# Where the group statistics and variances of the next image stand in the instruction order of an attention kernel

## The chip, the cores and the metric

The kernel runs on one core of one Trainium2 chip. The metric is the time of one execution in microseconds of the device. The time before is the median of four runs, 3243.06 us (3242.06 to 3248.0). The engines are called as in the profile: PE (matrix), PEld (its weight loads), DVE (vector), ACT (scalar), POOL (GpSimd), SP (the queue that issues most transfers).

## What is computed

Two layers of the same form over 4 images of 32 x 32 positions and 768 channels, all in float32:

```python
def _gn(v, G=32, eps=1e-5):
    g = v.reshape(B_, H_, W_, G, C_ // G)
    m = jnp.mean(g, axis=(1, 2, 4), keepdims=True)
    s = jnp.var(g, axis=(1, 2, 4), keepdims=True)
    return ((g - m) / jnp.sqrt(s + eps)).reshape(v.shape)

x = x + _L0_conv_ref(_gn(x), ...)
x = x + _L1_conv_ref(_gn(x), ...)
```

Each layer normalises 32 groups of 24 channels, makes q, k and v for 12 heads of 64, adds a bias of relative positions to the 1024 x 1024 scores of each head, takes a softmax, weighs v and projects the result, which is added to x. The second layer has biases on q, k and v and scales q once more.

## The kernel before

The four images of two layers make eight turns, called images 0 to 7 here; the result of one layer goes through DRAM (mid) and is the input of an image four turns later. An image has six pairs of heads (pair 0 to 5), and a pair has eight steps (n = 0 to 7), one for each block of 128 positions: 384 steps, all in one loop (L1005). The order is written out by hand: the order of the statements is the order of the instructions on each engine, and an engine runs its own in that order, waiting on semaphores for the others.

In a step, POOL makes the biases of the step two ahead (L536, tiles sc), PE the scores of the next step (L550), DVE adds the two and takes the row minimum (L562), ACT takes exponentials (L566) and, after a reciprocal on DVE (L573, in divide), scales the rows (L576). DVE transposes the scaled scores of the present step in blocks (L582, tile tb); SP sends them to DRAM (td<-tb, L584) and reads them back in another arrangement (pt<-td, L593) for PE to weigh v (L611), after which DVE evicts into attn (L620, L622).

Into these steps the loop lays the rest. Groups of matmuls (pj for q and k, pv for values, oa to od for the projection of the image before) follow the plans at L990 to L1001. Most groups are crossed: a first half of matmuls, then later a second half. To keep the second half from being moved up, DVE makes a tiny reduce of one column of the group's weights onto itself (between, L346: "wa<-wa", "wv<-wv" and so on): it waits for the first half, and the second half waits for it. These are the ordering instructions. The loop runs them for the groups in held at the start of the next step (L1048 to L1051), but not in steps 2 and 6. All groups take PSUM buffers of tag m, of which there are two; a group's buffer is free when DVE or ACT has evicted it (od: L736, then L733; oc: L733, then L736 twice, the last of which writes oy).

In step 7 the plan is the second half of an oc group or none, an od group, and the first half of the next q and k group (pj<-xn,wa). In step 0 it is the next od group, the second half of that pj group and a values group.

The norm of an image is made while the image before it runs. Its statistics (stats, L210 to L217: bn_stats of 512 columns each, then one bn_aggr) are put into at_stats for a step and run near the end of that step (L1116). At pair 3 the groups are summed on 32 x 32 blocks: group_means at the end of step 6 (L285, L286 and spread at L279, L280), squares on POOL (L290, L291), group_variances in step 7 (L279, L280, transposes L295 and L296, a sum L297, then the root on ACT, L298, which loads another table first), and inverses in step 0 of pair 4 (L301, L302). Group_variances and inverses stand behind the exponentials of their step and ahead of its matmul groups and transposes (L1070).

## Time and profile before

| What | Value |
|---|---|
| median of four runs | 3243.06 us |
| the profiled execution's own time | 3248.0 us |
| its span, first to last instruction | 3246.2 us |
| PE busy | 3218.7 us (99%) |
| DVE busy | 2578.9 us (79%) |
| ACT busy | 2093.4 us (64%) |
| POOL busy | 2572.1 us (79%) |
| DMA, mean rate | 317 GB/s |
| L298 table load, one | 1.283 us, 7 times |
| L214 bn_stats, one | 0.67 us (median), 96 times |

How to read it: busy times are sums of recorded instruction spans, and matmuls overlap in the record. A row of waits has the engine and line that waited, what ended the wait, the microseconds in total, the number of waits, and the longest. A row of the timeline has the start, the time taken, engine, line, operation, output and inputs, and in brackets the idle time of the engine before it and what ended it. L numbers are lines of the kernel.

### The profile page before, as it was taken

How to read it: one execution, taken by the hardware profiler on the slowest of the kernel's cores; microseconds unless marked ns; L12 is line 12 of the kernel's file. 1: busy time of each engine (PE TensorE's matmuls, PEld its weight loads, DVE VectorE, ACT ScalarE, POOL GpSimd, SP SyncE). 2: the span in 40 equal slices, each digit the busy share in tenths (PEclk: the TensorE clock that was granted, in tenths of full speed). 3: DMA queues.
4: the chain of work that ended last, by engine and by line, in shares of the span. 5: the costliest groups of instructions: out<-in, count | busy, mean ns of one | idle time of the engine just before them, and what ended most of it. 6: DMA issues, size and time to landing. Idle time of an engine off the chain costs nothing.

```text
span 3246.2 us, 63998 instructions
## 1 busy us (share of the span) xinstructions
PE 3218.7 (99%) x24800; PEld 1856.7 (57%) x24800; DVE 2578.9 (79%) x4085; ACT 2093.4 (64%) x3098; POOL 2572.1 (79%) x1364
## 2 busy tenths in 40 slices
PE   8999999999999999999999999999999999999999
PEld 5565556555555556555565555555565555555554
DVE  6888778887888877788777887778777788777785
ACT  4777766676566666667656676666766567665662
POOL 6888967789787797878978889777897778977762
PEclk9999999999999999999999999999999999999999
DMA  5998888999989998899988999789988899888996
GB/s 189 349 347 318 312 309 306 331 337 331 320 298 340 337 326 317 295 338 345 326 303 310 344 336 338 285 302 335 325 324 301 298 340 331 311 312 300 324 336 253
DMA packets 386847, 1028.84 MB, mean 317 GB/s; under 512 B 31344, under 2 KB 73200, under 8 KB 337392
## 3 DMA queue, kind: packets, MB, share of 16 engines
q1 hardware_dynamic: 370992, 997.33, 86.2%
q10 hardware_dynamic: 15552, 27.43, 2.3%
q8 instruction: 196, 3.21, 0.4%
q14 instruction: 107, 0.88, 0.1%
HBM read 566.93 MB, written 457.70 MB: 316 GB/s over the span
## 4 chain that ended last, share of the span: by engine, by line
PE 93%; DVE 3%; DMA 2%; issue 1%; ACT 0%; POOL 0%; SPq 0%; DVEq 0%; POOLq 0%
PE pj L357 22%; PE av L611 20%; PE s L550 20%; PE pv L357 11%; PE pj L385 4%; PE oa L357 3%; PE ob L357 3%; PE oc L357 3%; PE tp L488 2%; PE pv L441 2%; PE o L833 1%; PE od L719 1%; DVE tb L582 1%; DMA td<-tb 1%; DMA pt<-td 1%
## 5 line engine op out<-in xcount | busy, mean ns | idle before, releaser
L536 POOL TENSOR_TENSOR sc<-rel 128x1024 f32<-128x1024 f32 x768 | 1944.5, 2559 | 534.7 <-DVE tb L582 415.5
L576 ACT ACTIVATE sc<-sc,sm 128x1024 f32<-128x1024 f32 x768 | 841.0, 1143 | 592.6 <-DVE sm L573 478.5
L562 DVE CUSTOM_DVE_ANT_0 sc<-s,sc 128x1024 f32<-128x1024 f32 x768 | 910.7, 1225 | 338.2 <-PE s L550 325.0
L566 ACT ACTIVATE sc<-sc,sm 128x1024 f32<-128x1024 f32 x768 | 877.3, 1144 | 257.7 <-DVE sm L562 255.1
L582 DVE STREAM_TRANSPOSE tb<-sc 128x1024 f32<-128x1024 f32 x768 | 911.5, 1231 | 14.1 <-DMA td<-tb 14.1
L550 PE MATMUL s<-k,q 64*128 64x512 f32 x3072 | 736.4, 596 | 0.5 <-DVE k L401 0.5
L611 PE MATMUL av<-pt,v 128*64 128x256 f32 x6144 | 684.9, 381 | 1.2 <-DMA pt<-td 1.2
L611 PEld LDWEIGHTS av<-pt,v 128*64 128x64 f32 x6144 | 433.6, 137 | 281.7 <-issue 38.9
L550 PEld LDWEIGHTS s<-k,q 64*128 64x128 f32 x3072 | 285.0, 187 | 296.6 <-issue 263.5
L357 PEld LDWEIGHTS pv<-wv,xn 64*128 64x128 f32 x4608 | 271.3, 188 | 35.5 <-issue 29.4
L357 PE MATMUL pv<-wv,xn 64*128 64x128 f32 x4608 | 273.8, 272 | 0.5 <-DVE wv L346 0.5
L357 PE MATMUL pj<-xn,wa 64*128 64x512 f32 x1152 | 266.9, 595 | 4.7 <-DVE wa L346 2.6
L357 PE MATMUL pj<-s,wc 64*128 64x512 f32 x576 | 262.8, 589 | 0.6 <-DVE wc L346 0.6
L357 PE MATMUL pj<-s,w 64*128 64x512 f32 x576 | 262.8, 589 | 0.6 <-DVE v L459 0.6
L357 PE MATMUL pj<-xn,w 64*128 64x512 f32 x1152 | 263.2, 589 | 0.0
L357 PEld LDWEIGHTS pj<-xn,wa 64*128 64x128 f32 x1152 | 111.5, 188 | 142.0 <-issue 116.2
L357 PEld LDWEIGHTS pj<-xn,w 64*128 64x128 f32 x1152 | 112.0, 187 | 135.2 <-issue 133.1
L459 DVE TENSOR_TENSOR v<-pv,v 128x512 f32<-128x512 f32 x216 | 140.2, 686 | 59.4 <-ACT v L461 42.5
L493 ACT COPY t<-tp 128x512 f32<-128x512 f32 x96 | 56.2, 586 | 159.1 <-PE tp L488 159.0
L511 ACT COPY rel<-raw 32x256 f32<-32x256 f32 x384 | 154.7, 403 | 3.6
L357 PEld LDWEIGHTS pv<-wv,s 64*128 64x128 f32 x2304 | 137.0, 188 | 24.2 <-issue 16.9
L357 PEld LDWEIGHTS pj<-s,wc 64*128 64x128 f32 x576 | 105.8, 187 | 68.6 <-issue 64.6
(134 smaller groups left out, 3394.0 us busy)
## 6 DMA issues: line engine op xcount, KB each, us to landing
td<-tb SPq DMA_DIRECT2D x384, 1024.0 KB, 5.3
pt<-td SPq DMA_DIRECT2D x382, 1024.0 KB, 8.3
tdr<-t ACTq DMA_DIRECT2D x96, 256.0 KB, 5.4
wa<-in_wqk SPq DMA_DIRECT2D x48, 384.0 KB, 4.1
wc<-in_wqk SPq DMA_DIRECT2D x48, 384.0 KB, 5.7
wv<-in_wv SPq DMA_DIRECT2D x24, 768.0 KB, 12.0
xn<-in_x SPq DMA_DIRECT2D x48, 256.0 KB, 5.5
res<-in_x SPq DMA_DIRECT2D x48, 256.0 KB, 5.4
```

The source lines that it names most:

```text
L357: nc.tensor.matmul(to, lhsT=w, rhs=x, start=at == half == 0, stop=at == 0 and half == 1)
L385: nc.tensor.matmul(t[:, h, :], lhsT=w[rows, c, :], rhs=x[c][rows, :], start=(c == 0), stop=(c == NB - 1),)
L441: nc.tensor.matmul(t[:, h, b, :], lhsT=s4[c][rows, b * P : (b + 1) * P], rhs=w22[rows, c, :], start=(b, c) == (0, 0), stop=(b, c) == (3, N ...
L459: add = lambda to, x, y: nc.vector.tensor_tensor(to, x, y, ALU.add)
L511: nc.scalar.copy(rel[rows], raw[rows, :, :, WIDE - 1 - HW - y : WIDE - 1 - y])
L536: nc.gpsimd.tensor_tensor(sc.rearrange("p (a k) (u l) -> p a (k u) l", a=4, l=8), rel[:, h, m, :].unsqueeze(1).unsqueeze(3).to_broadcast(s ...
L550: nc.tensor.matmul(ps[h][:, cols], lhsT=q[rows, n * P : (n + 1) * P], rhs=k[rows, cols], start=True, stop=True,)
L562: nc.vector.tensor_tensor_reduce(out=sc, in0=ps[h], in1=sc, scale=-scale, scalar=BIG, op0=ALU.add, op1=ALU.min, accum_out=st[:, 0, h : h + 1],
L566: nc.scalar.activation(sc, sc, AF.Exp, bias=st[:, 0, h : h + 1], scale=-1.0, accum_out=st[:, 1, h : h + 1],)
L576: nc.scalar.mul(sc, sc, st[:, 2, h : h + 1])
L582: nc.vector.transpose(tb[:, :, h, :], sc_of[g, n, h])
L611: nc.tensor.matmul(av[rows, at * 2 * P : (at + 1) * 2 * P], lhsT=v_of[g][:, k, rows], rhs=pt_of[g, quarter].rearrange("p n r k h i -> p (n ...
```

## The change

Two moves, both of statements in the loop over steps.

First, the statistics of a step 7 are not run at the end of that step but at the start of the next one, after the ordering instructions of the held groups. On DVE this turns "bn_stats, reduce" into "reduce, bn_stats" at 14 boundaries between a step 7 and a step 0, with 18 bn_stats in all, in images 0 to 3. Statistics of other steps stay.

Second, group_variances of step 7 of pair 3 leaves its place behind the exponentials and runs near the end of the step, where group_means runs in step 6. On DVE its five instructions go from before the evictions of oc (images 1 to 6) and the two transposes (L582) to behind them and the reciprocal (L573), ahead of the evictions of the first od group and of the reduce of wa. On ACT the table load and the root of L298 go from before the two scalings (L576) to behind them. Inverses (L301, L302) stay in step 0 of pair 4. This happens seven times, for the norms of images 1 to 7.

The orders of PE, POOL and SP are unchanged, and so is the work of every engine.

```diff
@@ -1049,6 +1049,7 @@
                 for group in held:
                     group.between()
                 held = []
+            run(at_stats.pop(at - 1, []))
             run(at_start.pop(at, []))
             run(early)
             early, later = later, early
@@ -1067,7 +1068,7 @@
                 run(placing)
             run(behind[0])
             behind.append(behind.pop(0))
-            if (pair, n) in ((3, 7), (4, 0)) and not end:
+            if (pair, n) == (4, 0) and not end:
                 stages[n]()
             pieces = [now[name] for name in (plans[pair % 2] if g else first_plan).get(n, ()) if now.get(name)]
             if n == 0 and len(pieces) == 2:
@@ -1113,10 +1114,12 @@
                 if part[2] % 3:
                     combined(*part)
             run(at_sums.pop(at, []))
-            run(at_stats.pop(at, []))
-            if (pair, n) == (3, 6) and not end:
+            if n + 1 < NT:
+                run(at_stats.pop(at, []))
+            if pair == 3 and n in (6, 7) and not end:
                 stages[n]()
-                squares()
+                if n == 6:
+                    squares()
             if (n, pair % 2) == (3, 1):
                 for group in held:
                     group.between()
```

## The prediction

> **What bounds the kernel now.** I read the page's busy times first, then the chain that ended last, then what PE waited for, then the timelines of the places where the change moves instructions.

> ```profile
> PE 3218.7 (99%) x24800; PEld 1856.7 (57%) x24800; DVE 2578.9 (79%) x4085; ACT 2093.4 (64%) x3098; POOL 2572.1 (79%) x1364
> ...
> PE 93%; DVE 3%; DMA 2%; issue 1%; ACT 0%; POOL 0%; SPq 0%; DVEq 0%; POOLq 0%
> ```

> PE is idle for 3246.2 - 3218.7 = 27.5 us only, and 9.9 us of that is the first input (row PE spare L231 <- DMA xn<-in_x). The clock is granted in full in all 40 slices. So a reordering on DVE and ACT can win a few microseconds at most, and it costs only where it makes a PE wait. The waits of PE that touch the moved instructions:

> ```profile
> PE pj L357 <- DVE wa L346: 2.6, 7, 1.0
> PE pv L357 <- DVE wv L346: 2.1, 2, 1.5
> PE pj L357 <- DVE oy L736: 2.0, 3, 0.7
> PE av L611 <- DMA pt<-td: 1.2, 3, 0.4
> ```

> The reader is to see the times and counts in the last columns: seven waits for the ordering instruction of wa, three for the last eviction of oc (oy, L736).

> **What a PE wait costs.** A group of 12 matmuls takes 2.58 us to the next group (od starts at 2279.15, pj at 2281.73: 0.43 a pair), but a matmul is recorded with 0.59, so 0.16 of a wait hides under the last record; and a group after a wait lasts 2.85 us in the timeline against 2.74, 0.11 more. I count recorded gap + 0.27.

> **Part 1: the statistics (18 bn_stats at 14 step boundaries).** Each goes from before the ordering reduce (L346) of wa to behind it; 0.67 us recorded, 0.59 from start to start.

> ```profile
> 750.83 0.67 DVE L214 BATCH_NORM_STATS2 st<-res 128x6 f32<-128x512 f32 x1
> ...
> 751.42 0.14 DVE L346 TENSOR_REDUCE wa<-wa 128x1 f32<-128x1 f32 x1
> ...
> 751.61 0.70 PE L357 MATMUL pj<-xn,wa 64*128 64x512 f32 x2 [0.22 <-DVE wa L346]
> ```

> Here PE waits 0.22 for a reduce that a statistic delayed by 0.59, so the wait goes; the next DVE instruction, L562, starts when it did, since both stand before it either way. I looked at all 14 places. Four are like this (751, 1151, 1553, 1953; gaps 0.22 each): 4 x (0.22 + 0.27) = 1.95 us gained. Two lie in the first image (109, 227; gaps 0.36, worth 0.63 each), but there PE next waits for a read-back, at 126.05 and 243.66 (0.40 and 0.43), whose first transfer was issued at 108.80 and 226.38, ahead of the gain, and whose second was issued at 118.23 and 236.20. PE comes earlier and waits longer: 0. Eight have slack: in two PE reaches the reduced weights 1.5 us later, in six the reduce itself waits for PE and L562 then waits 1.66 us for scores, where one or two statistics (at most 1.24) fit. 0.

> **Part 2: the group variances at step 7 of pair 3, seven images.** Five small DVE instructions (L279, L280, L295, L296, L297) leave the place before the evictions of oc and the transposes (L582) and go behind the reciprocal (L573), just before the evictions of od (L736, L733). On ACT the table load and root (1.28 + 0.20) go behind the two scalings (L576); the inverses (L301) stay in step 0. No DMA moves; SP's and POOL's orders are as before.

> What is gained: at 680, 1080 and 1882 PE waits 0.747, 0.725 and 0.567 for oy, because the five stand before it and one of them is long:

> ```profile
> 675.01 2.57 POOL L536 TENSOR_TENSOR sc<-rel 128x1024 f32<-128x1024 f32 x1
> ...
> 676.18 1.43 DVE L280 TENSOR_SCALAR turned<-nrm 128x32 f32<-128x32 f32 x1
> ...
> 679.52 0.75 DVE L736 SCALAR_TENSOR_TENSOR oy<-oc,bo,oy 128x512 f32<-128x512 f32 x1
> ...
> 680.32 2.85 PE L357 MATMUL pj<-xn,wa 64*128 64x512 f32 x12 [0.75 <-DVE oy L736]
> ...
> 681.50 2.55 POOL L536 TENSOR_TENSOR sc<-rel 128x1024 f32<-128x1024 f32 x1 [3.92 <-DVE tb L582]
> ```

> L280 takes 0.18 us (median of 14) but 1.43 here: it ends at 677.61, 0.03 after the POOL instruction that was running. At 1076.47, 1479.13 and 1878.40 it does the same (1.41, 0.34, 1.25; each ends 0.03 to 0.04 after POOL's). So L280 is held while POOL runs L536. And POOL starts the next L536 when the first transpose ends: that is exactly where the change puts L280. After the change, the image 5 timeline must be read so:

> ```profile
> 2281.44 2.36 DVE L582 STREAM_TRANSPOSE tb<-sc 128x1024 f32<-128x1024 f32 x2
> ...
> 2282.76 5.06 POOL L536 TENSOR_TENSOR sc<-rel 128x1024 f32<-128x1024 f32 x2 [4.31 <-DVE tb L582]
> ...
> 2283.73 0.12 DVE L573 RECIPROCAL sm<-sm 128x2 f32<-128x2 f32 x1
> 2283.77 0.73 DVE L736 SCALAR_TENSOR_TENSOR ox<-od,bo,ox 128x512 f32<-128x512 f32 x1
> ...
> 2284.53 0.69 DVE L733 TENSOR_TENSOR ox<-od,ox 128x512 f32<-128x512 f32 x1
> ...
> 2286.02 2.74 PE L719 MATMUL od<-attn,wo_d 64*128 64x512 f32 x12
> ```

> Two od groups follow each other, and the second writes the PSUM buffer of the first (two buffers of tag m; pj holds the other), so PE at 2286.02 needs the L733 of 2284.53, done at 2285.22: 0.8 us of slack. Take T for the start of the transposes. Reciprocal T + 2.29; L279 T + 2.34; L280 starts at T + 2.55; POOL's first L536 runs from T + 1.32 to T + 3.87, so L280 ends at T + 3.91; from its end to the next DVE eviction 0.53 (677.61 to 678.14); L736 at T + 4.44, L733 at T + 5.20, done at T + 5.89; PE follows 0.05 later (as 680.32 follows 680.27): T + 5.94, where it ran at T + 4.57.

> In images 3, 5 and 6 T does not move, because the oc evictions start 0.24 us after PE's first od group anyway (2279.39 after 2279.15). Stall 1.37 + 0.11 = 1.48 each: **4.4 us lost**. In images 1, 2 and 4 the evictions move up to that point (677.07, 1077.36, 1879.29) and T to 679.11, 1079.40, 1881.33; the second od then starts at 685.05, 1085.34, 1887.27 instead of 684.72, 1084.98, 1886.75. With 0.11 each: 0.44 + 0.47 + 0.63 = **1.5 us lost**, the gain at oy already inside. In image 0 there is no od; L280 would end at 285.07, wa's reduce comes 0.19 late, but PE's next wait (1.53 at 294.37) hangs on ACT, whose scalings, two table loads and root now take from 285.43 to 290.43 instead of 290.32: 0.1 lost.

> The added wait: L301 needs the later root. In images 1 to 6 ACT has it at about T + 6.2, before DVE finishes the two L562 in front (T + 8.4): nothing. In image 0 L301 waits about 1.2 us, and the transposes behind it end near 291.9, before POOL (busy until 292.05) and before the next eviction, which waits for ACT until 293.2: nothing. The reduce of wa moves to T + 6.0, where PE wants it at T + 8.6. L562 moves 1.1 us later, less than PE. Each of these has cover of 0.4 us or more.

> **The sum:** 4.4 + 1.5 + 0.1 - 1.95 = +4.1 us, 0.13%. The profiled execution took 3248.0 us (span 3246.2), the slowest of four; its sum gives 3252.1. On the median of 3243.06 the same difference gives **3247.2 us**. About 0.2% (6.5 us) is what a measurement of this kernel can tell from no change, so I forecast no change, on the slow side.

> **The unknown, from both sides:** what L280 waits under two L536 in a row. Lower end: nothing (0.18, as at 2278.50 with POOL idle); the second od would start at T + 4.75, and the sum becomes 0.8 in images 3, 5, 6, -2.0 in 1, 2, 4, -1.95: -3.1 us. Upper end: it misses the boundary and waits for the second L536 too, 2.55 more. I take one L536: at 282.36 L280 got in between two L536 back to back (0.20 us, ending 0.04 after the first), and at 23.91 to 28.99 DVE's L326 alternate with POOL's one by one.

> [...]

> **Rivals.**
> *Slower by over 0.2%: L280 misses the boundary between the two L536.* Place: step 7 of pair 3, images 1 to 6. Price 2.55 each, 15.3 in all: 3262.5. It decides from the first image on (4.1 + 2.55 > 6.5). Against it: 282.36 and L326; for it: POOL's second L536 starts without a gap.
> *L280 isn't held there*, so that the change does what it looks like, taking DVE work out of PE's way: -3.1, 3240.0. Against it: four of four overlaps were held until POOL's end, except at the boundary.
> *The four gains of part 1 don't arrive*, eaten like those of image 0 by a later wait (1445.67 has one of 1.27 that began with a late DMA): +6.0, 3249.1.

> **Chances.** Forecast 0.70, boundary missed 0.08, not held 0.10, gains eaten 0.12. Over 0.2% slower (above 3249.5): 0.08, 0.07 of the eaten case, 0.12 of the forecast's own scatter (executions differ by 6 us): 0.27. Over 0.2% faster (below 3236.6): 0.03. Within: 0.70. Range: from the not-held case, 3239.5, to the eaten case with two images missing the boundary, 3249.1 + 5.1 = 3254.

> **What would show it.** In the changed profile: a new row of PE od L719 waiting for DVE ox L733, six times about 1.2 us recorded; the oy row gone; the wa row down from 7 waits to 1; L280 at about 1.36 us in six places behind the reciprocal; the pt row up to about 2.5. If L280 is short there, or no od waits, the step "L280 is held by POOL" or "the second od needs the first one's buffer" was wrong.

## The result, and the profile after

After the change the kernel takes 3250.45 us (median of 37 runs, 3246.06 to 3256.01); the kernel before, run beside it, takes 3246.67 (57 runs). The ratio is 1.0012, with a 95% interval of 1.0007 to 1.0017: slower by 3.8 us, between 2.3 and 5.5. The forecast of 3247.2 us stood on a median of 3243.06 for the kernel before, from four runs; from 57 it is 3246.67, so differences are compared here, not totals. The profiled execution took 3250.7 us, its span 3248.9 (before: 3248.0 and 3246.2).

The page of the changed kernel, busy times and chain of the work that ended last:

```profile
PE 3215.8 (99%) x24800; PEld 1854.1 (57%) x24800; DVE 2582.5 (79%) x4085; ACT 2093.2 (64%) x3098; POOL 2571.9 (79%) x1364
...
PE 93%; DVE 3%; DMA 2%; issue 1%; ACT 0%; POOL 0%; DVEq 0%; SPq 0%; POOLq 0%
```

Every engine has the same number of instructions, and the chain goes over PE as before. What differs is how long PE is idle: 33.1 us of the span instead of 27.5. (That is 5.6 us more, while the span grew by 2.7: in the first 300 us PE's recorded busy time fell from 283.4 to 280.3, since the start went otherwise. So I compare the starts of instructions below, not idle times.) The rows of PE's waits after the change (engine, line, what ended the wait: us in total, times, longest):

```profile
PE od L719 <- DVE wa L346: 7.2, 6, 1.2
PE av L611 <- DMA pt<-td: 2.9, 3, 2.0
...
PE pv L357 <- DVE wv L346: 2.0, 2, 1.5
PE pj L357 <- DVE wa L346: 1.2, 1, 1.2
```

A new row of six waits of od has come. Seven waits for wa have become one, and the row of oy is gone. The new waits sit where the prediction's T + 5.94 said. The timeline of image 5 after the change (T, the start of the transposes, is 2281.27):

```profile
2281.27 2.36 DVE L582 STREAM_TRANSPOSE tb<-sc 128x1024 f32<-128x1024 f32 x2
...
2282.58 5.01 POOL L536 TENSOR_TENSOR sc<-rel 128x1024 f32<-128x1024 f32 x2 [4.36 <-DVE tb L582]
...
2283.80 1.35 DVE L280 TENSOR_SCALAR turned<-nrm 128x32 f32<-128x32 f32 x1
...
2286.45 0.69 DVE L733 TENSOR_TENSOR ox<-od,ox 128x512 f32<-128x512 f32 x1
2287.06 0.14 DVE L346 TENSOR_REDUCE wa<-wa 128x1 f32<-128x1 f32 x1
2287.20 2.85 PE L719 MATMUL od<-attn,wo_d 64*128 64x512 f32 x12 [1.19 <-DVE wa L346]
```

L280 takes 1.35 us for 32 columns and ends at 2285.15, just after the first of POOL's two instructions (2282.58 + 2.53 = 2285.11). The eviction L733 comes late, and PE starts at 2287.20; T + 5.94 is 2287.21. The trace names the reduce of wa as what released PE. L733 ended 0.05 us before PE started, the reduce at the moment of the start; in nanoseconds, in all six places, L733 ended 53 or 54 ns before the start and the reduce 5 to 8 ns after it. That speaks for L733, and an experiment shows it (behind_od, below).

**Where the time went, term by term.** For each place, the start of the same PE instruction after the change minus before, taken against the difference just ahead of it:

| Place | Forecast, us | Traces, us |
|---|---|---|
| six od stalls, each | +1.37 + 0.11, with the oy gain inside in three | +1.35 to 1.37, + 0.10 or 0.11 |
| three oy waits (680, 1080, 1882) | -1.02, -1.00, -0.84 | -1.02, -1.00, -0.84 |
| four statistics (751, 1151, 1553, 1953) | -0.49 each | -0.49 each |
| sum of these | +4.0 | +4.0 |
| image 0 | +0.1 | +0.84 |
| late reads of before at 1445 and 1450 | none | -2.25 |

With 0.18 at 2234 (a wait for a read-back), the rows make up the 2.75 us between the two profiled executions. I put the last two differences down to chance: the execution before had waits of 1.27 and 0.59 us there, behind a read that came late (POOL's L536 at 1438.62 waited for it), and the one after has neither, and the first 300 us differ from trace to trace in how long PE waits for read-backs (at 300 us the eight new traces stand between -0.8 and +2.2 us against that of before).

### The profile page after: what moved, and what is told of

Read it like the earlier page. It is cut to its first block, busy times and chain, and to the rows that moved or that the text cites. A ratio compares the mean times of both kernels' runs of the same rounds, so it can differ in the third digit from the quotient of the medians.

```text
span 3248.9 us, 63999 instructions
## 1 busy us (share of the span) xinstructions
PE 3215.8 (99%) x24800; PEld 1854.1 (57%) x24800; DVE 2582.5 (79%) x4085; ACT 2093.2 (64%) x3098; POOL 2571.9 (79%) x1364
## 4 chain that ended last, share of the span: by engine, by line
PE 93%; DVE 3%; DMA 2%; issue 1%; ACT 0%; POOL 0%; DVEq 0%; SPq 0%; POOLq 0%
PE pj L357 22%; PE av L611 20%; PE s L550 20%; PE pv L357 11%; PE pj L385 4%; PE oc L357 3%; PE ob L357 3%; PE oa L357 3%; PE tp L488 2%; PE pv L441 2%; PE o L833 1%; PE od L719 1%; DVE tb L582 1%; DMA td<-tb 1%; DMA pt<-td 1%
## 5 line engine op out<-in xcount | busy, mean ns | idle before, releaser
L536 POOL TENSOR_TENSOR sc<-rel 128x1024 f32<-128x1024 f32 x768 | 1943.7, 2557 | 537.6 <-DVE tb L582 425.6
L576 ACT ACTIVATE sc<-sc,sm 128x1024 f32<-128x1024 f32 x768 | 841.1, 1143 | 598.1 <-DVE sm L573 459.1
L562 DVE CUSTOM_DVE_ANT_0 sc<-s,sc 128x1024 f32<-128x1024 f32 x768 | 910.6, 1224 | 323.9 <-PE s L550 309.1
L582 DVE STREAM_TRANSPOSE tb<-sc 128x1024 f32<-128x1024 f32 x768 | 911.0, 1229 | 16.4 <-DMA td<-tb 16.4
L611 PE MATMUL av<-pt,v 128*64 128x256 f32 x6144 | 684.9, 381 | 3.1 <-DMA pt<-td 2.9
L611 PEld LDWEIGHTS av<-pt,v 128*64 128x64 f32 x6144 | 433.5, 137 | 283.8 <-issue 40.5
L357 PEld LDWEIGHTS pv<-wv,xn 64*128 64x128 f32 x4608 | 271.2, 188 | 35.1 <-issue 27.9
L357 PE MATMUL pv<-wv,xn 64*128 64x128 f32 x4608 | 273.8, 272 | 0.5 <-DVE wv L346 0.5
L357 PE MATMUL pj<-xn,wa 64*128 64x512 f32 x1152 | 264.5, 590 | 1.9 <-DVE wa L346 1.2
L357 PE MATMUL pj<-s,w 64*128 64x512 f32 x576 | 264.0, 592 | 0.0
L357 PE MATMUL pj<-s,wc 64*128 64x512 f32 x576 | 264.0, 592 | 0.0
L357 PE MATMUL pj<-xn,w 64*128 64x512 f32 x1152 | 263.2, 589 | 0.0
L357 PEld LDWEIGHTS pj<-xn,w 64*128 64x128 f32 x1152 | 111.6, 187 | 135.6 <-issue 133.4
L357 PEld LDWEIGHTS pj<-xn,wa 64*128 64x128 f32 x1152 | 111.1, 187 | 135.9 <-issue 115.4
L357 PEld LDWEIGHTS pv<-wv,s 64*128 64x128 f32 x2304 | 137.1, 188 | 24.2 <-issue 17.0
L357 PEld LDWEIGHTS pj<-s,wc 64*128 64x128 f32 x576 | 106.3, 188 | 68.1 <-issue 64.8
```

Of the source, the lines that this page charges most:

```text
L357: nc.tensor.matmul(to, lhsT=w, rhs=x, start=at == half == 0, stop=at == 0 and half == 1)
L536: nc.gpsimd.tensor_tensor(sc.rearrange("p (a k) (u l) -> p a (k u) l", a=4, l=8), rel[:, h, m, :].unsqueeze(1).unsqueeze(3).to_broadcast(s ...
L562: nc.vector.tensor_tensor_reduce(out=sc, in0=ps[h], in1=sc, scale=-scale, scalar=BIG, op0=ALU.add, op1=ALU.min, accum_out=st[:, 0, h : h + 1],
L576: nc.scalar.mul(sc, sc, st[:, 2, h : h + 1])
L582: nc.vector.transpose(tb[:, :, h, :], sc_of[g, n, h])
L611: nc.tensor.matmul(av[rows, at * 2 * P : (at + 1) * 2 * P], lhsT=v_of[g][:, k, rows], rhs=pt_of[g, quarter].rearrange("p n r k h i -> p (n ...
```

## The experiments

The runs of the kernel before beside each experiment had a median of 3244.47 us for the first four and of 3245.18 for the last three (a different chip). "Outside image 0" is the sum of the differences of PE's starts from 300 us on, without 1445 and 1450, where the execution before had its late reads.

### stats_only: part 1 alone

```diff
+            run(at_stats.pop(at - 1, []))
             run(at_start.pop(at, []))
...
-            run(at_stats.pop(at, []))
+            if n + 1 < NT:
+                run(at_stats.pop(at, []))
```

> Part 1 alone: statistics behind the ordering reduces, group variances where they were. Theory (four gaps of PE at 751, 1151, 1553 and 1953 go, the two in image 0 are eaten by the read-back): -1.9 us against before, PE's row of waits for wa down from 7 to 1, the three waits for oy L736 still there. Rival (the gains are eaten later as well): 0. Rival (the statistics behind the reduce delay L562): slower.

Measured: 3244.83 us, ratio 0.9997 (0.9988 to 1.0006). The interval holds both the forecast of -1.9 us and nothing, so the time decides nothing. The trace does: PE's waits of this kernel keep the row of oy, while the row of wa has one wait left.

```profile
PE av L611 <- DMA pt<-td: 3.5, 2, 2.9
...
PE pj L357 <- DVE oy L736: 1.6, 3, 0.7
...
PE pj L357 <- DVE wa L346: 1.0, 1, 1.0
```

At 751, 1151, 1553 and 1953 PE comes 0.49 us earlier each time, as forecast. The rest of the difference between this trace and that of before is +0.84 in image 0 (the first row, with one read-back wait of 2.9), the late reads of before, and the oy waits. These are three again, but not the same three: the one of image 4 is gone (-0.84), since L280, held by POOL, took 0.50 us there instead of 1.25, and a new one of 0.16 stands in image 5 (+0.44), where L280 took 0.85 instead of 0.18. So in the old place L280 can be held for a different time in another execution; whether part 1 or chance moved it is not shown.

### variances_only: part 2 alone

```diff
-            if (pair, n) in ((3, 7), (4, 0)) and not end:
+            if (pair, n) == (4, 0) and not end:
...
-            if (pair, n) == (3, 6) and not end:
+            if pair == 3 and n in (6, 7) and not end:
                 stages[n]()
-                squares()
+                if n == 6:
+                    squares()
```

> Part 2 alone: group variances behind the reciprocal, statistics where they were. Theory (L280 is held by one L536 of POOL, the second od waits for the first one's eviction): +6.1 us against before, six waits of PE od L719 of 1.2 us recorded, no wait for oy, the six small waits for wa still there. Rival (the loss of the change comes from part 1): 0 or faster.

Measured: 3251.84 us, ratio 1.0024 (1.0014 to 1.0034), +7.8 us, with the forecast of 6.1 inside the interval. PE's waits in this kernel have the six od waits and the seven of wa, and none of oy:

```profile
PE od L719 <- DVE wa L346: 7.2, 6, 1.2
PE pj L357 <- DVE wa L346: 2.8, 7, 1.2
```

By PE's starts, the six od places lose 1.47 us each and the three oy places gain 2.86, as in the changed kernel: +6.0. The two parts act on different rows, and their shifts in the traces add up; the times do so only within their intervals (7.8 - 1.0 against 3.8). All of the loss is in part 2.

### after_free_spread: the change without the instruction that POOL holds

The long instruction of the five is the spread of the sums (L279 and L280: a reduce, then the tensor_scalar that was held). Here one reduce over a repeated input does both, the factor 1/n of the spread (a quarter) goes into L297, and EPS into the root's bias. ACT's order is that of the change.

```diff
+    eps = const.tile([P, 1], FP, tag="eps", name="eps")
+    nc.gpsimd.memset(eps, EPS)
...
-            spread(w1, w1)
+            nc.vector.tensor_reduce(
+                by_group(w2), by_group(w1).unsqueeze(2).to_broadcast([P, HW // n, n, n]),
+                mybir.AxisListType.X, ALU.add,
+            )
+            nc.vector.transpose(w1, w2)
             nc.vector.transpose(w2, w0)
-            nc.vector.transpose(w0, w1)
-            nc.vector.tensor_scalar(var, w2[:, 1:2], w0[:, 0:1], EPS, ALU.add, ALU.add)
-            nc.scalar.activation(inv, var, AF.Sqrt)
+            nc.vector.tensor_scalar(var, w1[:, 0:1], 1.0 / n, w2[:, 1:2], ALU.mult, ALU.add)
+            nc.scalar.activation(inv, var, AF.Sqrt, bias=eps)
```

> The changed kernel, but the variances are spread by one tensor_reduce over a repeated input, so that L280's tensor_scalar (the one that POOL holds) is gone there; the 1/4 goes into the sum of L297 and the epsilon into the root's bias. ACT's order stays that of the change. Theory (hold by POOL): the od waits shrink from 1.2 to 0.1 or vanish, -3.0 us against before. Rival (the loss comes from ACT, whose table load and root now delay the next exponentials): still +4 us, od waits gone or not.

Measured: 3244.71 us, ratio 0.9998 (0.9989 to 1.0006): -0.7 us, between -3.6 and +2.0. The expected -3.0 is inside, the change's own +3.8 is not. The timeline of image 5 in this kernel (lines are 5 later than in the change: L541 is POOL's L536, L738 is L733):

```profile
2277.61 5.05 POOL L541 TENSOR_TENSOR sc<-rel 128x1024 f32<-128x1024 f32 x2 [4.33 <-DVE tb L587]
...
2278.62 0.26 DVE L296 TENSOR_REDUCE turned<-turned 128x32 f32<-128x128 f32 x1
...
2279.41 0.21 DVE L302 TENSOR_SCALAR nrm<-turned,turned 128x1 f32<-128x1 f32 x1
...
2280.32 0.69 DVE L738 TENSOR_TENSOR ox<-od,ox 128x512 f32<-128x512 f32 x1
...
2281.06 2.85 PE L724 MATMUL od<-attn,wo_d 64*128 64x512 f32 x12
```

The same place beside the same two instructions of POOL costs DVE 0.26 us where L280 took 1.35. Od (L724) waits 0.03 us instead of 1.19 in each of the six places, where PE's starts come 0.2 us later instead of 1.47, and the row of oy stays away. So neither the place nor ACT's later root makes the loss, but one DVE instruction there that POOL holds. Outside image 0 PE's shift is -2.8 us.

### old_place_free_spread and old_place_again: the same reduce in the old place, with part 1

This is stats_only with the free spread, tried as a kernel that may be faster than before and after; the second run is the same kernel on the other chip.

> Part 1, and the group variances in their old place, spread without the tensor_scalar as in the run before this one. Theory: nothing is held in front of the oc evictions either, so the three waits for oy go (0.91 + 0.11, 0.88 + 0.11 and 0.73 + 0.11 us) and no od waits: -1.9 - 2.8 = -4.7 us against before. Rival (what the evictions of oc wait for is not the tensor_scalar): -1.9, oy waits still there.

Measured: 3243.12 us, ratio 0.9996 (0.9987 to 1.0004), -1.3 us. In the trace both the row of oy and that of od are gone, and outside image 0 PE gains 4.8 us, as expected; but in image 0 PE waited 2.13 and 2.95 us for read-backs (0.40 and 0.43 before).

> Statistics behind the reduces, variances in the old place without the held tensor_scalar, once more with five rounds, for a narrower interval together with the first time. Theory: -4.7 us of which image 0's read-back waits may give back up to 2.5 by chance; expected -2 to -5 us against before. Rival (no gain reaches the end): 0.

Measured: 3242.42 us, ratio 0.9989 (0.9980 to 0.9997): -3.6 us. PE's waits in this execution; the waits for read-backs (L616 is L611) are again the largest after the first input:

```profile
PE av L616 <- DMA pt<-td: 4.4, 4, 2.3
PE pv L362 <- DVE wv L351: 2.4, 3, 1.6
```

The second interval excludes no change, the first doesn't. Outside image 0 this trace gains 4.3 us. The mean of the two ratios is 0.9992, about -2.5 us: perhaps the fastest of these kernels, by less than 0.2%, but the intervals of stats_only and after_free_spread hold 0.9992 too.

### behind_od: does od wait for L733 or for wa?

The five instructions stand behind the evictions of the first od group and the reduce of wa, last in the step.

```diff
-            if pair == 3 and n in (6, 7) and not end:
+            if (pair, n) == (3, 6) and not end:
                 stages[n]()
-                if n == 6:
-                    squares()
+                squares()
...
             for k in range(done, len(pieces)):
                 run_part(k)
+            if (pair, n) == (3, 7) and not end:
+                stages[n]()
```

> The changed kernel, with the group variances behind the evictions of the first od group as well (last in step 7). Theory (the second od needs the buffer that the first od's L733 frees, not the reduce of wa that the profile names): no od waits, though the reduce of wa comes 3.3 us later than before the change; L280 is now held by the second L536, the next eviction (second od) is late instead, and PE waits for it ahead of the values group, six times 1.4 us recorded: +5 us against before. Rival (od waits for the reduce of wa): six od waits of 2.5 us, +12 us or more.

Measured: 3252.99 us, ratio 1.0024 (1.0015 to 1.0033), +7.8 us; the expected 5 is at the interval's lower end, and the trace's shift outside image 0 is 5.6. PE's row of the new wait, and the timeline of image 5 in this kernel:

```profile
PE pv L357 <- DVE ox L733: 7.7, 6, 1.3
```

```profile
2284.49 5.03 POOL L536 TENSOR_TENSOR sc<-rel 128x1024 f32<-128x1024 f32 x2 [4.33 <-DVE tb L582]
...
2286.26 0.69 DVE L733 TENSOR_TENSOR ox<-od,ox 128x512 f32<-128x512 f32 x1
...
2287.08 2.48 DVE L280 TENSOR_SCALAR turned<-nrm 128x32 f32<-128x32 f32 x1
2287.75 2.74 PE L719 MATMUL od<-attn,wo_d 64*128 64x512 f32 x12
...
2290.09 0.14 DVE L346 TENSOR_REDUCE wa<-wa 128x1 f32<-128x1 f32 x1
...
2294.41 0.83 PE L357 MATMUL pv<-wv,s 64*128 64x128 f32 x10 [1.28 <-DVE ox L733]
```

Od starts without a wait at 2287.75, 0.8 us after L733 has ended and 2.3 us before the reduce of wa runs. So od does not need the reduce of wa; in the changed kernel it waited for L733 to free the PSUM buffer, although the trace named the reduce. And L280, begun 0.04 us after POOL's first instruction had ended, is held through the whole second one (2.48 us, to 2289.56; POOL ends at 2289.52). The delay comes out as a wait of PE later on, for the evictions of the next od group, six times 1.28 us.

### twice_held: two held instructions

The tensor_scalar of the spread is executed twice, with the same result.

```diff
-            spread(w1, w1)
+            total = work[:, : HW // n]
+            nc.vector.tensor_reduce(total, by_group(w1), mybir.AxisListType.X, ALU.add)
+            for _ in range(2):
+                nc.vector.tensor_scalar(
+                    by_group(w1), total.unsqueeze(2).to_broadcast([P, HW // n, n]), 1.0 / n, None, ALU.mult
+                )
```

> The changed kernel with L280 of the group variances executed twice (the second writes the same values). Theory (each execution is held until the L536 that runs at its start ends): the second is held by the second L536, 2.55 us more in six images, od waits of 3.7 us recorded, +19 us against before. Rival (only the first instruction after the transposes is slow, or the hold is a fixed delay of switching): +5 to +6 us, the second execution takes 0.2 us.

Measured: 3275.66 us, ratio 1.0089 (1.0074 to 1.0105), +28.9 us where 19 was expected; the rival's 5 to 6 is out. The timeline of image 5 in this kernel (5 lines later again; L297 is the doubled instruction, L724 is od):

```profile
2301.34 5.02 POOL L541 TENSOR_TENSOR sc<-rel 128x1024 f32<-128x1024 f32 x2 [4.34 <-DVE tb L587]
...
2302.55 3.84 DVE L297 TENSOR_SCALAR turned<-nrm 128x32 f32<-128x32 f32 x2
...
2308.44 2.85 PE L724 MATMUL od<-attn,wo_d 64*128 64x512 f32 x12 [3.68 <-DVE wa L351]
```

Both copies together take 3.84 us: the first gets in at the boundary between POOL's two instructions, the second waits for the end of the second, 2.44 us longer. Od's wait grows from 1.19 to 3.68, by 2.49. That is the price of the rival "misses the boundary" (2.55 in the prediction). It gives 6 x 2.49 = 14.9 us on top of the change; most of the rest is PE's clock, for which the windows of this kernel at image 1 are shown (us of the window, us; busy time of PE, PEld, DVE, ACT, POOL; granted clock; DMA share; GB/s):

```profile
684.00:688.70 4.70, 1.02 (x6) 0.49 (x6) 4.60 (x8) 2.91 (x4) 3.80 (x3) 1.00 1.00 309
688.70:692.10 3.40, 3.40 (x10) 1.37 (x8) 1.81 (x6) 2.38 (x4) 0.00 (x0) 0.50 1.04 387
692.10:696.00 3.90, 3.90 (x35) 2.28 (x33) 3.44 (x4) 0.59 (x1) 0.71 (x1) 1.00 0.52 191
```

After the wait that ended at 687.93, PE ran at clock 0.50 for 3.4 us. Four of the six od waits have such a spell behind them, 20.5 us in all; at a clock of 0.50 I estimate 10.2 us for them, and PE's starts after them are 9.1 us later than in the changed kernel. In image 0 the wait for wa (3.72 us instead of 1.22) and a fifth spell cost 2.3 us, after a later wait for ACT has taken up a part. 3.8 + 14.9 + 9.1 + 2.3 = 30.1, near the 28.9.

## Why the prediction was right

The total was +4.1 us and came out as +3.8 (2.3 to 5.5). It was right by its steps: the forecast terms, read one by one in the traces, sum to the +4.0 of the table. That the two profiled executions differ by only 2.75 us is chance, since +0.84 and -2.25 that nobody forecast stand beside these terms. The prediction called the change too small to tell from none (6.5 us); 57 and 37 runs could tell 3.8. Its range begins at 3239.5, where its own sum for "not held" gives 3240.0; no step rests on that.

- **L280 is held by POOL's L536, and gets in at the boundary between two.** Predicted 1.36 us in six places, found 1.35 to 1.38 in images 1 to 6, each ending 0.03 to 0.04 us after POOL's first instruction. The rival "not held" fell with this row, and after_free_spread shows what it would have looked like. The rival "boundary missed" fell too; its cost is real, as twice_held shows, but DVE, which was already waiting, got its turn at the boundary each time.
- **The second od needs the buffer of the first.** Six stalls of 1.47 us; behind_od shows that it is L733 and not the reduce of wa. The prediction expected the trace to name L733; it named the reduce of wa, which ended 0.06 us later.
- **The oy waits go, at 0.75, 0.73 and 0.57 plus 0.27.** Found to 0.01 us. The rule "recorded gap plus 0.27" held in all three and in the four statistics. But these three gaps are those of one execution of before; in stats_only, with the same place for L280, they were 0.74, 0.74 and 0.16. That the change removes them is shown, that they are worth 2.86 us in every execution is not.
- **Part 1 gives 4 x 0.49.** Found in the trace of the change and in that of stats_only; not resolved in time (0.9988 to 1.0006). The rival "gains eaten" fell outside image 0.
- **Image 0 gives nothing back.** It went as predicted in kind: PE was 0.53 us earlier at 109.5, and at 126 its read-back wait grew. But the size was off: the row of pt was forecast at 2.5 and is 2.9, with one wait of 2.0 instead of 0.40. In seven of the eight new traces such a wait is 2.0 to 2.95 us long, more than PE was early, so it is not only the gain eaten. Nor does the change make them: variances_only, with before's order of instructions up to 282 us, has one of 2.49. The traces of before (0.43 at most) and of twice_held (1.0 at most) are the two without. What makes the read-backs late was not tried.

Two expectations of the experiments were mis-sized: twice_held by the clock (28.9 against 19), and the free spreads in time (-0.7 against -3.0, and -1.3 against -4.7; the second run of the latter, -3.6, lay in its expected -2 to -5), though the traces outside image 0 gave -2.8, -4.8 and -4.3. Where the difference lies is not shown: image 0 stood at -0.8, +1.3 and +2.2 us in these three traces, and the scatter of the runs is as large as the effect.

## What to carry to other kernels

Before moving small instructions behind a long one, look at what the other engine starts at that moment: a DVE instruction of 0.18 us became one of 1.35 here because the end of the first transpose starts POOL as well. Change the instruction rather than the place: the reduce of 0.26 to 0.28 us that POOL did not hold took the waits of PE away in both places (od 0.03 us, no oy row). And where two possible releasers end within 0.1 us of a start, don't trust the one that the trace names; compare their ends with the start, move one of them and see.

## What the runs showed of the hardware

**Who gets in between two POOL instructions.** When L280 was waiting as one L536 ended, with the next ready, it was let in between them each time: six times in the change, in its image 0 (285.38 to 285.76, POOL's end 285.73), and six times in twice_held. Where it came 0.04 us after that end, as in behind_od, it was held for the whole next one, 2.48 us, six times.

```profile
30.80:34.20 3.40, 3.40 (x20) 1.88 (x18) 0.00 (x0) 2.20 (x6) 2.69 (x3) 0.50 0.21 77
34.20:40.00 5.80, 5.80 (x30) 2.71 (x28) 0.31 (x2) 0.31 (x1) 0.00 (x0) 1.00 0.31 90
```

The granted clock is 0.50 in the first window and 1.00 in the next. A spell costs 3.4 x 0.5 = 1.7 us, an estimate that twice_held bears out: behind the spell at 688.66 PE's starts are 1.7 us later, against the change, than ahead of it. So a wait may cost more than its length.

In five of these waits it went with where they lay. The changed kernel's spell lies from 30.80 to 34.21, 3.413 us. In twice_held spells begin at 285.89, 688.66, 1091.43, 1497.62 and 1903.80, that is 118, 118, 119 and 119 times 3.413 us apart. Counted in steps of 3.413 us from the start of a spell, forwards and back, the wait of 2.03 us that ended at 30.23 lies in one step, and the next is at 0.50; the one of 2.02 that ended at 127.42 lies across a border, with 1.05 us in the longer part, and the clock stays at 1.00. In twice_held the waits that ended at 687.93 and 1498.29 have 2.68 and 3.00 us in one step, and a spell follows; the one of 3.68 that ended at 2308.44 has 1.81 and 1.87 us on the two sides of a border, and the clock behind it is 1.00. How much idle time in a step it takes is not shown beyond these five.

The clock goes with part of the scatter: of the changed kernel's runs, with the profiled one, 17 with a mean clock of 0.999 have a median of 3252.1 us, 21 with 1.0 one of 3249.2.
